# One gated attention and feed-forward block on one core: each engine's instructions kept in the written order, every step in a slot of its own

## The chip, the cores and the metric

The kernel runs on one core of one Trainium2 chip. The metric is the device time of one execution in microseconds, the median of several runs. The engines are named as in the profile: PE (TensorE; PEld its weight loads), DVE (VectorE), ACT (ScalarE), POOL (GpSimd) and SP, whose queue issues most DMAs. POOL issues the indirect DMAs. A line such as L619 is a line of the kernel before.

## The reference, cut to what matters

There are 8 batches of 256 rows, 512 channels, 16 heads of 32; the feed-forward is 1408 wide.

```
x = x + tanh(g_xattn) * xattn(layernorm(x), ctx, mask)
x = x + tanh(g_ffn)   * ffn(layernorm(x))

xattn: q = w8a8_linear(xn, wq, bq)             # rows and weights rounded to int8 with a scale a row
       k = ctx @ wk.T + bk ; v = ctx @ wv.T + bv                            # fp32
       a = softmax(q k.T / sqrt(32) + mask)    # 256 x 256 for each of 16 heads
       return w8a8_linear(a v, wo, bo)
ffn:   xr = x / scale; xr = xr[:, up_reorder_index]       # rows put on an fp8 grid
       g = qlinear(xr, w_gate) ; u = qlinear(xr, w_up)    # columns in down_reorder_index order
       t = silu(g) * u                                    # put on the fp8 grid again, a scale a row
       return qlinear(t[:, down_reorder_index], w_down)
```

The maximum over a row of t (1408 numbers) must be known before that row's grid can be made, and all of attention's output row before it can be rounded to int8.

## The kernel before, in words

Rows are tiled by 128, so a batch has two row tiles. The program is written in a tile framework: its scheduler orders the instructions of each engine when the program is built, from priorities and a timing model of its own, and each engine then works through its queue in that fixed order. The one order that is written by hand is that of the score products and of the head products (`in_turn`).

The outer loop runs over 8 batches of 8 pairs of heads, plus 8 further turns. A turn issues `scores`, `transposed` and `products` of three successive pairs, and then a list of helper steps that `spread` hands out over the turns of a batch: the next batch's norm, keys, values and queries, the last batch's output projection and second norm, a third of the weight pieces in each of batches 0 to 2, and feed-forward steps from batch 3 on.

```
for lag in range(3):
    if 0 <= g - lag < B * NP:
        parts[(g - lag) // NP][lag]((g - lag) % NP)
for f in slots[i]:
    f()
```

The steps and lines that are spoken of below:

| step | lines and tiles |
|---|---|
| softmax of one head | L578 PE scores s (4 banks, one buffer, for 4 heads); L593 DVE sn = -(s + mask) with its row minimum nm; L603 ACT exponential pr with its row sum |
| turning the probabilities | L619 PE transposes t of fp32; L628 DVE (even heads) and L626 ACT (odd heads) copy to pT |
| products with the values | L637 PE poT, four heads in one bank; L651 ACT copy oT; L654 PE transposes po; L658, L660 DVE normalise into o |
| keys, values | L463 PE ct, L466 ACT cT; L473 PE pk, L480 ACT kT; L489 PE pv, L496 DVE v |
| queries | L514 ACT, L522 DVE round; L524 PE qt, L529 copy; L535 PE pq, L542 DVE qT, L545 POOL adds the bias |
| output projection | L299, L300 DVE round o; L687 PE ot, L692 copy; L698 PE py, L706 DVE y; L709, L710 POOL add to x; L711 SP stores x1 |
| second norm | L724 to L729 DVE; L158, L160 ACT and L162, L163 DVE put rows on the fp8 grid; L306 PE transposes tb_x, L309 copy; SP stores scr_x |
| feed-forward, a unit of 352 columns | L752 POOL gathers xg; L775 PE gate and up; L786 DVE scales both; L795 ACT tanh; L796, L797, L798 POOL make tt |
| feed-forward, the end of a row tile | L180 DVE row maximum mxt; L158 to L163 the grid qt; L306 PE tb_t, L309 copy qtT; L828 PE yp; L834 DVE yo; L835 POOL adds x1; SP stores out |
| weight pieces | L395 POOL gathers rows, L401 POOL masks them, then maximum, grid, L306 transposes; the weights go to HBM (scr_gate, scr_up, scr_d) and come back in the wanted order by indirect DMA |

All PE results other than the scores share one ring of four PSUM banks (`bank`, tag m). A row tile of feed-forward has one buffer for tt, qt and qtT each. Copies written `nc.any` may be placed on ACT or DVE by the scheduler. x has four buffers, pr five, pT six, the bf16 rows q8 two, the fp32 rows r_v four.

Of the kernel before, what the change touches and what calls it, by code (L numbers as in the profile page):

```python
# [40 lines left out]
P = 128  # L41
# [8 lines left out]

@with_exitstack
def tile_flamingo_block(
# [22 lines left out]
    nc = tc.nc  # L75
    B, S, C = x.shape
    L = cond.shape[1]
    I = w_gate.shape[0]
    H = 16
# [42 lines left out]
    zeros = ctile([P, IC], "zeros")  # L122
    nc.vector.memset(zeros, 0.0)
    ones = ctile([P, 1], "ones")
    nc.vector.memset(ones, 1.0)
# [25 lines left out]
    held_d = [dram.tile([I, 1], F32, tag=f"held{k}", name=f"held{k}") for k in range(IC)]  # L151
# [3 lines left out]
    def fp8_grid(rp, src, rs, dst, n, name):  # L155

        v = rp.tile([P, n], F32, tag="r_v", bufs=4, name=f"v_{name}")
        nc.scalar.activation(v, src, AF.Identity, scale=rs)  # L158
        a = rp.tile([P, n], FP8, tag="r_a", name=f"a_{name}")
        nc.scalar.activation(a, v, AF.Abs, scale=0.5, saturate=False)  # L160
        q = rp.tile([P, n], FP8, tag="r_q", name=f"q_{name}")
        nc.vector.tensor_scalar(q, v, F8_MAX, -F8_MAX, ALU.min, ALU.max, saturate=False)  # L162
        nc.vector.scalar_tensor_tensor(dst, a, F8_MAX / 2, q, ALU.max, ALU.mult)  # L163

    def scale_of(pool, mx, s, name):

        nc.vector.tensor_scalar(s, mx, R448, None, ALU.mult)  # L167
        rs = pool.tile([P, s.shape[-1]], F32, tag="rs", name=f"rs_{name}")
        nc.vector.reciprocal(rs, s)  # L169
        return rs  # L170

    def int8_scale(pool, mx, s, name):

        nc.vector.tensor_scalar(s, mx, R127, Q_EPS, ALU.mult, ALU.max)
        rs = pool.tile([P, s.shape[-1]], F32, tag="rs8", name=f"rs8_{name}")
        nc.vector.reciprocal(rs, s)
        return rs

    def absmax(dst, src):
        nc.vector.tensor_reduce(dst, src, AX.X, ALU.max, apply_absolute_value=True)  # L180

    with ExitStack() as actx:
# [15 lines left out]

        xt = {}
        norm1, norm2 = {}, {}  # L200

        def load_x(b):
            xt[b] = ld.tile([P, TPB, C], F32, tag="x", name=f"x_{b}", bufs=4)
            nc.sync.dma_start(xt[b], x[b].rearrange("(t p) c -> p t c", p=P))

        def row_tile(b, name, n=1):
            return sm.tile([P, n * TPB], F32, tag=name, name=f"{name}_{b}", bufs=3)

        def norm_stats(b):
            mv = sm.tile([P, TPB, 2], F32, tag="mv1", name=f"mv1_{b}", bufs=3)  # L210
            for nt in range(TPB):
                st = sm.tile([P, 6], F32, tag="st", name=f"st1_{b}_{nt}")
                nc.vector.bn_stats(st, xt[b][:, nt, :])
                nc.vector.bn_aggr(mv[:, nt, :], st)
            norm1[b] = mv

        def norm_roots(b1, b2):

            r = row_tile(b1, "rstd", 2)
            todo = []  # L220
            if b1 < B:
                todo.append((r[:, :TPB], norm1[b1][:, :, 1]))
            if b2 >= 0:
                todo.append((r[:, TPB:], norm2[b2][:, :TPB]))
            for to, var in todo:
                nc.vector.tensor_scalar(to, var, LN_EPS, None, ALU.add)
            ra = r[:, : TPB if b2 < 0 else None] if b1 < B else r[:, TPB:]
            nc.scalar.activation(ra, ra, AF.Sqrt)
            nc.vector.reciprocal(ra, ra)
            if b2 >= 0:  # L230


                s_x = row_tile(b2, "s_x", 2)
                nc.vector.scalar_tensor_tensor(
                    s_x[:, :TPB], norm2[b2][:, TPB:], UNIT, r[:, TPB:], ALU.mult, ALU.mult
                )
                nc.vector.tensor_scalar(s_x[:, TPB:], s_x[:, :TPB], 0.5, None, ALU.mult)
                norm2[b2] = s_x
            if b1 < B:
                nmean = row_tile(b1, "nmean")  # L240
                nc.vector.tensor_scalar(nmean, norm1[b1][:, :, 0], -1.0, None, ALU.mult)
                norm1[b1] = r[:, :TPB], nmean, row_tile(b1, "sx")

        def norm_max(b, nt):
            _, nmean, sx = norm1[b]
            xc = rp.tile([P, C], F32, tag="r_v", bufs=4, name=f"xc_{b}_{nt}")
            nc.scalar.activation(xc, xt[b][:, nt, :], AF.Identity, bias=nmean[:, nt : nt + 1])
            absmax(sx[:, nt : nt + 1], xc)

        def norm_scales(b):  # L250
            rstd, nmean, sx = norm1[b]
            qa, qb = row_tile(b, "qa"), row_tile(b, "qb")
            nc.vector.tensor_tensor(sx, sx, rstd, ALU.mult)
            nc.vector.tensor_scalar(sx, sx, R127, Q_EPS, ALU.mult, ALU.max)
            nc.vector.reciprocal(qa, sx)
            nc.vector.tensor_tensor(qa, qa, rstd, ALU.mult)
            nc.vector.tensor_tensor(qb, qa, nmean, ALU.mult)
            norm1[b] = sx, qa, qb

        def norm_steps(b):  # L260

            steps = [partial(norm_stats, b), partial(norm_roots, b, b - 3)]
            steps += [partial(norm_max, b, nt) for nt in range(TPB)]
            return steps + [partial(norm_scales, b)]


        wT8 = {}
        s8 = {}
        for n, w in (("q", wq), ("o", wo)):
            wT8[n] = wp.tile([P, KC, C], BF16, tag=f"w{n}T", name=f"w{n}T")  # L270
            s8[n] = wp.tile([P, KC], F32, tag=f"s_{n}", name=f"s_{n}")
        wTf = {n: wp.tile([P, KC, C], F32, tag=f"w{n}T", name=f"w{n}T") for n in ("k", "v")}

        def load_halves(n, w, tag):

            halves = []
            for i in range(2):
                wr = kv.tile([P, 2, C], F32, tag=tag, name=f"wr_{n}{i}")
                nc.sync.dma_start(
                    wr, w[i * 2 * P : (i + 1) * 2 * P, :].rearrange("(k p) c -> p k c", p=P)  # L280
                )
                halves.append(wr)
            return [halves[k // 2][:, k % 2, :] for k in range(KC)]

        def prep_fp32(n, rows):
            for k in range(KC):
                wr = rows[k]
                pt = bank(f"pt_{n}{k}")
                for cc in range(KC):
                    nc.tensor.transpose(  # L290
                        pt[:, cc * P : (cc + 1) * P], wr[:, cc * P : (cc + 1) * P], ident
                    )
                nc.scalar.copy(
                    wTf[n][:, :, k * P : (k + 1) * P], pt.rearrange("p (c o) -> p c o", o=P)
                )

        def round_int8(src, rs, dst, name):
            w = rp.tile([P, C], F32, tag="r_v", bufs=4, name=f"ri_{name}")
            nc.vector.tensor_scalar(w, src, rs, MAGIC, ALU.mult, ALU.add)  # L299
            nc.vector.tensor_scalar(dst, w, -MAGIC, None, ALU.add)  # L300

        def transpose_bf16(src, dst, n, name):

            pt = bank(f"tb_{name}", BF16)
            for k in range(n):
                nc.tensor.transpose(  # L306
                    pt[:, k * P : (k + 1) * P], src[:, k * P : (k + 1) * P], ident_b
                )
            nc.any.tensor_copy(dst, pt[:, : n * P].rearrange("p (k o) -> p k o", o=P))  # L309

        def load_rows(n, w, tag, bufs):

            tiles = []
            for k in range(KC):
                wr = at.tile([P, C], F32, tag=tag, name=f"wr_{n}{k}", bufs=bufs)
                nc.sync.dma_start(wr, w[k * P : (k + 1) * P, :])
                tiles.append(wr)
            return tiles

        def prep_int8(n, tiles):  # L320
            for k, wr in enumerate(tiles):
                sk = s8[n][:, k : k + 1]
                absmax(sk, wr)
                rs = int8_scale(sm, sk, sk, f"w{n}{k}")
                qw = at.tile([P, C], BF16, tag="q8", name=f"qw_{n}{k}")
                round_int8(wr, rs, qw, f"w{n}{k}")
                transpose_bf16(qw, wT8[n][:, :, k * P : (k + 1) * P], KC, f"w{n}{k}")

        def row_bcast(dst, cols, name):

            n = cols.shape[-1]
            for k0 in range(0, n, 4):
                m = min(4, n - k0)
                pb = bank(f"rb_{name}{k0}")
# [11 lines left out]
        def held_up():  # L346
# [8 lines left out]
            for k in range(KC):  # L355
# [4 lines left out]
                )  # L360
            nc.vector.tensor_scalar(mu_b, pc, 1.0, None, ALU.min)

        marks = []

        def mark_down(k):

# [636 lines left out]
```

## Time and profile before

| what | us |
|---|---|
| median of three runs | 896.36 |
| lowest, highest | 893.34, 897.14 |
| profiled execution, whole | 906.7 |
| its span | 904.9 |
| first exponential, last exponential of attention | 64.1, 762.8 |
| busy PE, DVE, ACT, POOL | 571.7, 579.7, 443.4, 395.1 |
| mean granted clock of PE | 0.791 of full |

A row of a group of instructions gives line, engine, operation, result and operands, count, busy time and the mean duration of one. A row of waits gives who waited for whom, the sum, the number of times and the longest. A row of stretches gives the stretch, its length, then for each engine the busy time and the number of instructions, the granted clock, the DMA share and GB/s. Rows of the timeline give start, duration, engine, line, operation and operands.

### The profile page before, as it was taken

Reading aid. Unit: us, or ns where it says so; the run is one execution under the profiler, and the core shown is the slowest. Engines: PE = TensorE matmul, PEld = TensorE weight load, DVE = VectorE, ACT = ScalarE, POOL = GpSimd, SP = SyncE. Lnnn points to the kernel's source line nnn. Section 1 sums busy time; section 2 is a strip of 40 time slices with the busy share of each in tenths; the row PEclk is TensorE's granted clock in tenths of the full one; section 3 lists DMA queues with packets and bytes.
Section 4 is the critical chain, followed back from the end, with each engine's and each line's share of the span. In section 5 each row is a group of like instructions: output and inputs, shape, how many; then the busy total and the mean of one; then the engine's idle time right before and its main releaser. Section 6 shows DMA issues by size and latency. Waiting matters only on the chain.

```text
span 904.9 us, 11148 instructions
## 1 busy us (share of the span) xinstructions
PE 571.7 (63%) x3571; PEld 364.4 (40%) x3594; DVE 579.7 (64%) x1645; ACT 443.4 (49%) x1066; POOL 395.1 (44%) x396
## 2 busy tenths in 40 slices
PE   2577785668773679476857677586954765652342
PEld 2436464445542446243524354354533433321121
DVE  3558696597887477646766755866774776555332
ACT  1448675368466464445544543574452545224121
POOL 4374524343300655433625272543617246544650
PEclk9777899787876789677968797887968788765775
DMA  8412132123313301110001101010101001110100
GB/s 258 118 49 64 54 123 88 35 90 138 119 65 124 107 1 48 47 44 21 34 33 58 47 13 36 23 37 12 36 20 40 23 25 40 31 46 12 36 12 13
DMA packets 32898, 50.17 MB, mean 55 GB/s; under 512 B 8411, under 2 KB 15963, under 8 KB 32838
## 3 DMA queue, kind: packets, MB, share of 16 engines
q1 hardware_dynamic: 24598, 36.70, 12.0%
q0 software_dynamic: 4656, 12.21, 4.8%
q10 hardware_dynamic: 3584, 0.54, 0.5%
q8 instruction: 28, 0.46, 0.2%
q14 instruction: 32, 0.26, 0.1%
HBM read 34.55 MB, written 14.88 MB: 55 GB/s over the span
## 4 chain that ended last, share of the span: by engine, by line
PE 26%; POOL 21%; DVE 21%; issue 15%; ACT 10%; DMA 4%; ACTq 1%; another core or an unknown queue 1%; POOLq 0%; DVEq 0%
PE yp L828 6%; POOL tt L798 5%; POOL th L796 5%; POOL th L797 5%; PE pk L473 4%; PE pv L489 3%; PE t L619 3%; DVE mxt L180 3%; DMA wr_gate<-in_L_ffn_w_gate_dram,dd_i 2%; ACT pr L603 2%; DVE sn L593 2%; POOL xg L752 2%; PE poT L637 2%; DVE qt L163 1%; ACT v_t L158 1%
## 5 line engine op out<-in xcount | busy, mean ns | idle before, releaser
L603 ACT ACTIVATE pr<-sn,nm 128x256 f32<-128x256 f32 x256 | 127.9, 501 | 59.3 <-DVE nm L593 21.0
L593 DVE CUSTOM_DVE_ANT_0 sn<-s,mk 128x256 f32<-128x256 f32 x256 | 98.2, 417 | 21.1 <-ACT pr L603 11.4
L795 ACT ACTIVATE th<-gate 128x352 f32<-128x352 f32 x64 | 31.8, 497 | 118.8 <-DVE gate L786 87.4
L619 PE MATMUL t<-ident,pr 128*128 128x128 f32 x512 | 85.9, 322 | 5.6 <-DVE qT L542 4.1
L796 POOL TENSOR_SCALAR th<-th 128x352 f32<-128x352 f32 x64 | 71.4, 1116 | 34.9 <-ACT th L795 26.2
L545 POOL TENSOR_SCALAR qT<-qT,bq_c 128x256 f32<-128x256 f32 x32 | 17.1, 533 | 153.8 <-DVE qT L542 101.6
L473 PE MATMUL pk<-cT,wkT 128*128 128x256 f32 x256 | 71.6, 437 | 17.4 <-ACT cT L466 8.1
L835 POOL TENSOR_TENSOR x<-x,yo 128x512 f32<-128x512 f32 x16 | 20.4, 1276 | 141.1 <-DVE yo L834 140.7
L619 PEld LDWEIGHTS t<-ident,pr 128*128 128x128 f32 x512 | 73.8, 171 | 11.9 <-DVE qT L542 4.3
L306 PE MATMUL tb_t<-ident_b,qt 128*128 128x128 bf16 x176 | 25.0, 301 | 83.3 <-DVE qt L163 81.8
L180 DVE TENSOR_REDUCE mxt<-tt 128x1 f32<-128x1408 f32 x16 | 25.9, 1620 | 76.7 <-POOL tt L798 76.7
L775 PEld LDWEIGHTS <-xg 128*128 128x128 bf16 x512 | 53.3, 105 | 43.5 <-issue 9.8
L473 PEld LDWEIGHTS pk<-cT,wkT 128*128 128x128 f32 x256 | 55.6, 225 | 27.2 <-ACT cT L466 8.3
L828 PE MATMUL yp<-wdT,qtT 128*128 128x512 bf16 x163 | 60.7, 537 | 6.3 <-ACT qtT L309 5.2
L489 PE MATMUL pv<-wvT,cT 128*128 128x512 f32 x128 | 64.1, 648 | 0.5 <-DVE gate L786 0.5
L158 ACT ACTIVATE v_t<-tt,rs_t 128x512 f32<-128x512 f32 (+1 forms) x48 | 31.0, 675 | 67.3 <-DVE rs_t L169 44.0
L797 POOL TENSOR_TENSOR th<-th,gate 128x352 f32<-128x352 f32 x64 | 60.3, 942 | 4.8
L798 POOL TENSOR_TENSOR tt<-th,up 128x352 f32<-128x352 f32 x64 | 59.8, 935 | 4.3
L775 PE MATMUL p_gate<-gateT,xg 128*128 128x352 bf16 x256 | 54.6, 337 | 5.1 <-issue 3.6
L775 PE MATMUL p_up<-upT,xg 128*128 128x352 bf16 x256 | 54.4, 337 | 3.5 <-issue 3.5
L578 PE MATMUL s<-kT,qT 32*128 32x256 f32 x512 | 43.3, 459 | 20.7 <-DVE n L167 8.1
L786 DVE SCALAR_TENSOR_TENSOR gate<-p_gate,s_x,sb_gate 128x352 f32<-128x352 f32 x64 | 37.1, 579 | 29.6 <-POOL th L797 15.0
(193 smaller groups left out, 1350.7 us busy)
## 6 DMA issues: line engine op xcount, KB each, us to landing
x<-x SPq DMA_DIRECT2D x32, 256.0 KB
cr<-in_ctx_dram SPq DMA_DIRECT2D x8, 512.0 KB
x<-in_x_dram SPq DMA_DIRECT2D x8, 512.0 KB
out_dram<-x SPq DMA_DIRECT2D x16, 256.0 KB
wd<-in_L_ffn_w_down_dram SPq DMA_DIRECT2D x4, 704.0 KB
mk<-in_mask_BxSxS_ff_dram SPq DMA_DIRECT2D x8, 256.0 KB
scr_x<-x2T SPq DMA_DIRECT2D x8, 256.0 KB
scr_gate<-gateT SPq DMA_DIRECT2D x1, 1408.0 KB
```

The lines of the kernel that those rows point to most:

```text
L180: nc.vector.tensor_reduce(dst, src, AX.X, ALU.max, apply_absolute_value=True)
L473: nc.tensor.matmul(pk[:, :L], wTf["k"][:, cc, oc * P : (oc + 1) * P], cT[:, cc, :], start=(cc == 0), stop=(cc == KC - 1),)
L489: nc.tensor.matmul(pv, cT[:, cc, lt * P : (lt + 1) * P], wTf["v"][:, cc, :], start=(cc == 0), stop=(cc == KC - 1),)
L578: return nc.tensor.matmul(pss[h][:, nt, :], qT[r0 : r0 + D, oc, nt * P : (nt + 1) * P], kT[r0 : r0 + D, oc, :], start=True, stop=True,)
L593: nc.vector.tensor_tensor_reduce(out=sn[:, nt, :], in0=pss[h][:, nt, :], in1=mk[:, nt, :], scale=-1.0, scalar=3.0e38, op0=ALU.add, op1=ALU ...
L603: nc.scalar.activation(pr[:, nt, :], sn[:, nt, :], AF.Exp, bias=nm[:, nt : nt + 1], scale=-1.0, accum_out=sums[:, nt, h : h + 1],)
L619: nc.tensor.transpose(pst[:, lc, nt * P : (nt + 1) * P], pr[:, nt, lc * P : (lc + 1) * P], ident,)
L775: nc.tensor.matmul(ph[n], xg[0][:, k, nt * P : (nt + 1) * P], wT[n][:, k, cols], start=(k == 0), stop=(k == KC - 1),)
L796: nc.gpsimd.tensor_scalar(th, th, 1.0, None, ALU.add)
L797: nc.gpsimd.tensor_tensor(th, th, scaled["gate"], ALU.mult)
L798: nc.gpsimd.tensor_tensor(h["tt"][:, cols], th, scaled["up"], ALU.mult)
L828: nc.tensor.matmul(py, h["qT"][:, k, :], wdT[:, k, :], start=(k == 0), stop=(k == IC - 1))
```

## The change

`InOrder` wraps each engine; once switched on, it marks every instruction to stay in the order in which it is written, on its engine. The prologue, up to the queries of batch 0, is still ordered by the scheduler.

The loop over turns becomes a loop over 83 slots. The first 64 belong to the 64 pairs of heads. `early(g, step)` and `late(g, step)` enter a step in an agenda, in front of the softmax of slot g or at its end. A slot issues in this order: scores (every other slot, for four heads), early steps, the softmax of its pair, head products of the pair three slots back, transposes of the pair one slot back, normalising of the pair four slots back, late steps. Every chain is cut where it changes engine: a grid, for example, becomes `grid_parts` (ACT), `grid_whole` (DVE) and the transposes (PE), in successive halves of slots.

```diff
+class InOrder:
+    def __getattr__(self, name):
+        method = getattr(self.engine, name)
+        def issue(*args, **kwargs):
+            ins = method(*args, **kwargs)
+            return self.tc.keep_in_program_order(ins) if self.on else ins
+        return issue
...
-for g in range(B * NP + NP):
-    b, i = divmod(g, NP)
-    if i == 0:
-        slots = [[] for _ in range(NP)]
...
-            spread(slots, norm_steps(b + 1), 0, 3)
-            spread(slots, kv_steps, 0, 6)
-            spread(slots, q_steps, 3, 7)
...
-            spread(slots, project_out(b - 1, o_last) + quantise_x2(b - 1), 2, NP)
...
-    for lag in range(3):
-        if 0 <= g - lag < B * NP:
-            parts[(g - lag) // NP][lag]((g - lag) % NP)
-    for f in slots[i]:
-        f()
+for e in (pe, dve, act, pool, sp):
+    e.on = True
+for g in range(max(s for s, _ in agenda) + 1):
+    b, i = divmod(g, NP)
+    if b < B and i % PPC == 0:
+        scores(b, i // PPC)
+    for f in agenda.get((g, 0), []):
+        f()
+    if b < B:
+        softmax(b, i)
+    for lag, f in ((3, weighted), (1, transposed), (4, normalised)):
...
+    for f in agenda.get((g, 1), []):
+        f()
```

A feed-forward row tile and the steps after a batch's attention, with the slots that the rest is built on:

```
# feed_forward(b, nt, g)                      # follow(b, g): projection and second norm
if nt == 0: early(g - 1, gather_x, b)         early(g, rounded)
for j in range(4): late(g + j // 2, unit, j)  late(g + 1, turned)
early(g + 2, scales)                          for nt in range(TPB): late(g + 2, product, nt)
late(g + 2, parts, 0); late(g + 2, parts, 1)  early(g + 3, centred, 0); late(g + 3, parts, 0)
early(g + 3, parts, 2)                        early(g + 4, whole, 0); early(g + 4, centred, 1)
early(g + 3, whole, 0); early(g + 3, whole, 1) late(g + 4, back, 0); late(g + 4, parts, 1)
late(g + 3, turned, 0); late(g + 3, whole, 2) early(g + 5, whole, 1); late(g + 5, back, 1)
late(g + 3, load_x1)                          late(g + 5, store)
late(g + 4, turned, 8); late(g + 5, down)
...
for k in range(IC): up_piece(k, k)            # one gate piece and one up piece a slot, slots 0 to 12
for k in range(KC): down_piece(k, IC + 2 + 2 * k)
for k, (b, nt) in enumerate(ahead): feed_forward(b, nt, 25 + 10 * k // 3)   # batches 0 to 5
for nt in range(TPB):
    feed_forward(B - 2, nt, B * NP + 3 + 3 * nt)
    feed_forward(B - 1, nt, B * NP + 10 + 3 * nt)
```

In batch b's eight slots the next batch's work lies thus: the norm in slots 1 and 2, context transposes late in 0 and 1, keys in 1 and 2, values in 3 and 4, rows of queries in 2 and 3, queries in 4 and 5; the last batch's `follow` starts in slot 3.

Further edits:

- The weights wv and wo are prepared in slots 0 to 2 in place of ahead of the first scores; gate and up pieces are made two a slot in place of one after the other, and their marks (an indirect DMA a piece) with them.
- Copies of turned rows that were `nc.any` are ACT's; of each pair of weight pieces, up's is DVE's. The two normalising products of a group of heads are one instruction.
- Weight loads of w_down are issued by POOL in place of SP. The marks and their zero tables are bf16, and their rows are loaded in slot 10.
- Buffers: x 3, pr 4, pT 5, q8 5, the fp32 rows 4 for ACT's and 2 for DVE's, sn 4 of half the size. The ring of four PSUM banks, the score banks and the single tt, qt and qtT stay.

## The prediction

> **What bounds the kernel now.** I read the page's head first: which engines are busy, the granted clock, the chain that ended last.
>
> ```profile
> span 904.9 us, 11148 instructions
> PE 571.7 (63%) x3571; PEld 364.4 (40%) x3594; DVE 579.7 (64%) x1645; ACT 443.4 (49%) x1066; POOL 395.1 (44%) x396
> PEclk9777899787876789677968797887968788765775
> PE 26%; POOL 21%; DVE 21%; issue 15%; ACT 10%; DMA 4%; ACTq 1%; another core or an unknown queue 1%; POOLq 0%; DVEq 0%
> ```
>
> No engine is above 64%, and the chain passes from engine to engine with none over 26%: the kernel is bound by hand-offs in fixed queues, not by an engine. Second, the span cut at the first exponential (64 us), at batches and at the last one (763 us):
>
> ```profile
> core 0: us, PE busy (x) PEld busy (x) DVE busy (x) ACT busy (x) POOL busy (x), PEclk, DMA share, GB/s
> 64.00:124.00 60.00, 44.44 (x318) 32.08 (x320) 45.98 (x145) 44.12 (x117) 29.56 (x28) 0.86 0.20 61
> 385.00:488.00 103.00, 70.75 (x449) 44.14 (x454) 63.98 (x179) 51.40 (x126) 41.83 (x42) 0.80 0.12 39
> 591.00:675.00 84.00, 61.77 (x407) 40.17 (x403) 57.96 (x172) 46.21 (x118) 37.16 (x38) 0.85 0.07 23
> 763.00:882.00 119.00, 52.94 (x283) 27.32 (x285) 58.35 (x120) 33.38 (x57) 66.27 (x65) 0.69 0.09 29
> ```
>
> A batch (eight pairs of heads) takes 60 us while it carries little else and 84 to 103 us beside feed-forward, though DVE, the fullest, is busy 58 to 64 us of that. Third, the waits, who waited for whom:
>
> ```profile
> PE tb_t L306 <- DVE qt L163: 81.8, 20, 15.1
> DVE mxt L180 <- POOL tt L798: 76.7, 16, 8.6
> DVE yo L834 <- PE yp L828: 50.0, 15, 5.3
> PE tb_x L306 <- DVE q L163: 49.9, 11, 9.9
> PE po L654 <- ACT oT L651: 29.3, 28, 6.1
> PE tb_d L306 <- DVE q_d L163: 20.8, 8, 8.8
> ```
>
> Each is an instruction standing in its queue right behind what makes its operand on another engine: a transpose behind its quantisation, the row maximum behind POOL's last product. Everything queued behind it waits too. Fourth, the timeline, for the pitch of instructions that follow each other (start to start), which is what they occupy:
>
> ```profile
> 61.97 0.42 DVE L593 CUSTOM_DVE_ANT_0 sn<-s,mk 128x256 f32<-128x256 f32 x1
> 62.31 0.42 DVE L593 CUSTOM_DVE_ANT_0 sn<-s,mk 128x256 f32<-128x256 f32 x1
> 873.01 1.09 POOL L796 TENSOR_SCALAR th<-th 128x352 f32<-128x352 f32 x1
> 876.09 1.09 POOL L796 TENSOR_SCALAR th<-th 128x352 f32<-128x352 f32 x1
> ```
>
> sn lasts 417 ns but comes every 345; a unit of feed-forward costs POOL 3.07 us.
>
> **What the Trainium skill says.** (1) "TensorE: Matmul & The Clock Gate", Part 1: TensorE runs at half clock unless recent windows of about 3.4 us were busy. The trace agrees: pitch of the transposes of L619 is 213 ns in half-clock stretches, 109 in full ones; mean granted clock 0.79. (2) Same page, "Architectural detail: the array is 16× 32×32": ScalarE and VectorE are strict first-in-first-out, TensorE pulls only weight loads ahead. The mxt row agrees: 76.7 us with DVE standing. (3) "Perfetto Trace Analysis", "Optimizing Scalar/DVE Operations": an instruction's profiled duration overlaps its successor; 417 against 345 agrees. I count with pitches.
>
> **The change, part by part.** *Work.* It hardly changes. DVE loses the bf16 copies the scheduler gave it (qtT 3.2, x2T 2.5, upT 1.7 of which it keeps half the pieces, qoT 2.8 us) and saves about 2 us by one normalising product in place of two; ACT gains about 10. Counting the written order of the new program with pitches of before (PE at full clock: L619 109 ns, key and value products 216 and 429 per record, gate and up 149, down 216; DVE sn 345, pT 602, gate and up 500, mxt 1540 to 1560, grid 335+602; ACT exponential 400+93) gives for the 64 slots of a pair: PE 358 us (421 at clock 0.85), DVE 449, ACT 363, POOL 318. Table loads (1.28 us each, about 20 before) stay: still one square root per batch.
>
> *Order.* The written order is kept from the first slot on; before it the scheduler still places. A slot has a front (scores, early steps, softmax, lagged transposes and head products) and a back (late steps). The front is DVE's: 320 us of it against PE 112, ACT 186. The back is PE's: 246 at full clock against DVE 129, ACT 177; POOL has 261 there. Worked for slot 26 (batch 3): front DVE = norm_end 1.9 + 4 sn 1.4 + pT 0.6 + normalising 0.45 = 4.4, PE = 8 score records, 8+2 transposes = 1.9; back PE = 2 key products 3.4 + 2 units 2.4 = 5.8, DVE = 4 scalings 2.0, ACT 3.0, POOL 6.0. The fullest engine needs 7.7, both parts one after the other 10.1.
>
> Why they hardly overlap: DVE and ACT empty PE's four ring banks in order, so PE does its front and about one late product, then stands until pT and the copies of that slot are made; DVE reaches its late steps when PE has just begun. So I sum over 64 slots front maximum plus back maximum: 605 us at full clock, 642 at 0.85, 661 at 0.79. I take 0.85 (the windows at 591 and 64 us, where PE was about as full). From it: PE's head start, about 1 us a slot (two transposed heads and one product), -64. Hand-offs inside a slot not hidden, 0.5 us (some four at 0.1 to 0.2 as the short gaps of PE before L828 and L775 show), +32. The row maximum of a tile stands early in the slot after its last two units: POOL ends 7.4 us after the first of these scalings starts (0.5 + 0.5 + 2 x 3.07 + hand-offs), DVE is through after 2.4 and has about 1.8 us of other early steps: 3 us wait less PE's slack, 12 tiles x 2.5 = +30 (56 in this stage before). Square root slots: two table loads in front of the exponentials, 8 x 2.6, half hidden, +10. Sum **650 us**, 10.2 a slot; before 763 - 64 = 699.
>
> *Start.* Scores come right after the queries; before, DVE's qT waited for the transposes of wv (3.0 + 1.7 us) and sn stood behind a weight piece and the next norm until 61.97 though scores ran at 54.85. First exponential about 53 us in place of 64; the moved wv and wo work is in the slots' sums.
>
> *End.* Before, 763.3 to 904.9 = 142 us. After: lags and gather until tile (6,0)'s first unit 14 (4 from the last exponential, 10 through follow's store, gather, landing); its POOL units 12.3; maximum, grids, and the next tile's first unit, because tt has one buffer and PE's transposes stand before the units, 8; (6,1) 12.3; gather of batch 7, 4.2 issue and landing, first unit, 12; (7,0) with one residual addition and half-clock PE 15.6; 8.5; (7,1) 12.3; from its last tt to the end 22.7 as before (882.2 to 904.9). Sum **118**.
>
> *At nothing.* Marks and zero tables in bf16; w_down's loads on POOL's queue (four, in slots where POOL has 1 to 5 us of work); the 11 single-row loads of the marks on SP at slot 10 (before, 16 us of issues from 41 to 57): behind them SP has a load of ctx used four slots later, the two weight stores and x1 stores; if the rows land late, held_down at slot 12 holds PE's queue once, up to 5 us (in the range). SP's other loads and stores stand one to four slots ahead of their users. Smaller rings (x 3, pr 4, pT 5): what frees each stands a slot earlier. POOL's three-operation gathers are 3 us in slots whose POOL sum is 5.6 of about 9; if that cover goes, DVE's mx_gate waits, up to 3 us in 11 slots. Bounds for the hand-offs, which the trace of before does not show in this order: 0 to 1.5 us a slot (0 to 96); for the head start 0 to 2.
>
> Total 53 + 650 + 118 = 821 against its own 904.9 (906.7 with what lies around the span). The median of the runs shown is 896.36, 8.5 under the span, so 821 - 8.5 = **813**.
>
> **Rivals.** (a) *Slots run at their fullest engine.* If four banks and a slot's slack suffice, the sum is of slot maxima: 528 at 0.85, +40 for maxima and table loads = 568; 53 + 568 + 112 - 8.5 = 725. For: slack of a slot between most steps. Against: one ring of four banks for every product. (b) *Slower: the clock.* Every slot has a front in which PE has 1.7 us of work and stands for 2 to 3. If this keeps the clock low, the backs double: two-part sums 755 at 0.6, 838 at 0.5. It decides in the attention slots: break-even is 904.9 - 53 - 118 = 734, that is 726 before corrections, at a mean granted clock of about 0.65. At 0.6: 763, in all 925. For: 0.69 in the tail, where PE is 44% busy. Against: PE would then be over 80% busy and earn full clock back; 0.80 to 0.86 in the batches. (c) *Waits only change place.* Maxima still stand behind POOL and yo behind yp; with 0.9 us of hand-offs (+58), no head start and the +30 the slots take 642 + 58 + 30 = 730: 893. For: those two rows were 127 us before. Against: the four transpose rows are separated by at least half a slot now.
>
> **How the numbers follow.** Forecast 0.66, (a) 0.14, (b) 0.12, (c) 0.08, split evenly between slower by more and the rest. About 0.5%, 4.5 us, is what a measurement of this kernel can tell from no change (three runs lie within 3.8 us). Forecast and (a) are faster: 0.80; within 0.5% 0.04; slower 0.16. The range takes (a)'s upper half to just above no change: 740 to 905; without (b) and (c) the forecast's own is 760 to 870.
>
> **What would show it.** Right: first exponential near 53 us, batches of 75 to 90 us each, the transpose rows of the waits (tb_t, tb_x, tb_d) down to a few us, DVE near 65 to 70% of the stage, PE standing in fronts with pT or a copy as releaser, mxt <- tt still 30 to 50 us. Wrong: clock under 0.7 between 53 and 700 us (b); batches under 72 us (a); mxt or yo waits over 100 us (c).

## The result and the profile after

The changed kernel takes 934.79 us, median, against 896.75 for the kernel before on the same chip: a ratio of 1.042 (95% interval 1.037 to 1.047). It is **slower by 4%**, where 813 was predicted. The profiled execution took 933.0 us, 931.2 of them its span. In the profile of a kernel with `InOrder` nearly every instruction bears the line of the wrapper (L61, or L62 where an experiment added a line), so it is read by tiles.

The head of the page, the same rows as before:

```profile
span 931.2 us, 11038 instructions
PE 583.0 (63%) x3570; PEld 366.7 (39%) x3591; DVE 605.6 (65%) x1590; ACT 463.2 (50%) x1092; POOL 402.7 (43%) x400
PEclk9978877887878598778987699888878777677775
DVE 34%; PE 25%; POOL 15%; ACT 11%; issue 9%; DMA 3%; another core or an unknown queue 1%; POOLq 0%; DVEq 0%; ACTq 0%; SPq 0%
```

The mean clock (0.798; 0.791 before) is what it was, and the engines' busy times are up by 2 to 5%. Of the chain, DVE's share has grown most, from 21 to 34%. The stretches, with the columns as before, are batches 0, 4 and 6 and the end:

```profile
38.30:135.20 96.90, 63.12 (x374) 41.29 (x373) 73.20 (x200) 54.74 (x130) 54.90 (x49) 0.82 0.21 63
411.50:517.10 105.60, 67.98 (x436) 41.87 (x439) 66.74 (x179) 49.72 (x124) 47.40 (x47) 0.86 0.10 33
610.30:712.10 101.80, 70.34 (x437) 44.34 (x439) 66.49 (x179) 51.21 (x126) 40.45 (x42) 0.82 0.07 24
797.70:905.00 107.30, 56.82 (x277) 29.48 (x282) 58.57 (x120) 43.40 (x76) 63.94 (x62) 0.73 0.11 35
```

By its first and last exponential the execution splits into 39 us of start (64 before), 760 of slots (699) and 132 of end (142). Start and end gained 35 us, the slots lost 61. The loss lies in batches 0 to 2, which carry the weight pieces: 97, 93 and 92 us, counted from first sn to first sn, against 61, 73 and 80; the other five, up to the last sn, together take 5 us more than before. (By sn the slots lost 72 us; before, the last exponential came 13 us after the last sn, now 1.) Part of it is moved work, since weights that were prepared ahead of the first scores are now made in the slots. The two rows are batches 0 to 2, before and after:

```profile
62.00:276.20 214.20, 155.03 (x1028) 106.71 (x1029) 168.54 (x510) 139.35 (x353) 77.59 (x73) 0.83 0.27 86
```

```profile
38.30:319.40 281.10, 181.72 (x1123) 120.79 (x1124) 199.06 (x552) 159.18 (x386) 107.13 (x102) 0.79 0.25 82
```

DVE is busy there for 31 us more, and for 14 less ahead of them. But even from the beginning of the execution to the end of batch 2 it is 319 us, where it was 276, and in no batch of the changed kernel was an engine busy for more than 76% of the time. So the answer is in the waits:

```profile
ACT pr L61 <- DVE nm L61: 249.9, 51, 12.9
...
DVE mxt L61 <- POOL tt L61: 56.7, 14, 6.3
PE tb_t L61 <- DVE qt L61: 52.0, 15, 14.6
...
DVE gate L61 <- PE p_gate L61: 43.2, 27, 5.0
DVE yo L61 <- PE yp L61: 41.7, 11, 7.0
PE tb_up L61 <- DVE pT L61: 34.2, 9, 5.6
...
PE tb_x L61 <- DVE q L61: 9.6, 10, 2.9
```

The rows that the change was cut for did go: tb_x 49.9 to 9.6, and of tb_t's 52.0 only 7.5 are in the slots. New ones stand in their place. PE products of every sort (tb_up is one of a dozen) stand for DVE's **pT**, which must empty a bank of their ring: summed over the slots 163 us of the 253 in which PE waited. DVE, in turn, stands before the instructions that take PE's late products (gate, yo, v; called takers below). Both happen in one slot of the timeline:

```profile
525.51 0.75 DVE L61 SCALAR_TENSOR_TENSOR yo<-yp,sy,sd_b 128x512 f32<-128x512 f32 x1 [5.60 <-PE yp L61]
...
531.78 0.69 DVE L61 COPY pT<-t 128x512 f32<-128x512 f32 x1
...
532.52 3.78 PE L61 MATMUL pk<-cT,wkT 128*128 128x256 f32 x8 [3.30 <-DVE pT L61]
...
538.37 0.58 DVE L61 SCALAR_TENSOR_TENSOR gate<-p_gate,s_x,sb_gate 128x352 f32<-128x352 f32 x1 [4.97 <-PE p_gate L61]
```

From 525.5 to 533 DVE does the norm's statistics, two grids, four sn and pT without a pause, and PE stands for 3.3 us of it; then PE runs its products and DVE stands for 5. The two engines take turns.

### The profile page after: what moved, and what is told of

Same layout as the page of the kernel before. It is cut to its first block, busy times and chain, and to the rows that moved or that the text cites. A ratio compares the mean times of both kernels' runs of the same rounds, so it can differ in the third digit from the quotient of the medians.

```text
span 931.2 us, 11038 instructions
## 1 busy us (share of the span) xinstructions
PE 583.0 (63%) x3570; PEld 366.7 (39%) x3591; DVE 605.6 (65%) x1590; ACT 463.2 (50%) x1092; POOL 402.7 (43%) x400
## 4 chain that ended last, share of the span: by engine, by line
DVE 34%; PE 25%; POOL 15%; ACT 11%; issue 9%; DMA 3%; another core or an unknown queue 1%; POOLq 0%; DVEq 0%; ACTq 0%; SPq 0%
POOL th L61 8%; PE pk L61 6%; DVE sn L61 6%; PE pv L61 5%; POOL tt L61 4%; ACT pr L61 4%; PE yp L61 3%; DVE mxt L61 3%; POOL x L61 2%; PE p_gate L61 2%; DVE pT L61 2%; DVE qt L61 2%; DVE up L61 2%; PE p_up L61 2%; DVE q_up L61 1%
## 5 line engine op out<-in xcount | busy, mean ns | idle before, releaser
L61 ACT ACTIVATE pr<-sn,nm 128x256 f32<-128x256 f32 x256 | 126.9, 497 | 255.1 <-DVE nm L61 249.9
L61 POOL TENSOR_SCALAR th<-th 128x352 f32<-128x352 f32 x64 | 73.4, 1146 | 186.0 <-ACT th L61 142.2
L61 DVE CUSTOM_DVE_ANT_0 sn<-s,mk 128x256 f32<-128x256 f32 x256 | 92.8, 418 | 13.9 <-remote 8.1
L61 PE MATMUL pk<-cT,wkT 128*128 128x256 f32 x256 | 77.4, 464 | 30.4 <-DVE pT L61 14.8
L61 PEld LDWEIGHTS <-xg 128*128 128x128 bf16 x512 | 58.0, 115 | 58.8 <-issue 17.3
L61 PE MATMUL t<-ident,pr 128*128 128x128 f32 x512 | 78.7, 302 | 3.5 <-ACT x2T L61 1.4
L61 PEld LDWEIGHTS pk<-cT,wkT 128*128 128x128 f32 x256 | 58.3, 236 | 44.5 <-DVE pT L61 16.8
L61 PEld LDWEIGHTS t<-ident,pr 128*128 128x128 f32 x512 | 62.2, 154 | 32.3 <-issue 12.2
L61 PE MATMUL p_gate<-gateT,xg 128*128 128x352 bf16 x256 | 63.2, 378 | 16.3 <-DVE pT L61 13.1
L61 DVE SCALAR_TENSOR_TENSOR gate<-p_gate,s_x,sb_gate 128x352 f32<-128x352 f32 x64 | 37.3, 582 | 49.4 <-PE p_gate L61 43.2
L61 PE MATMUL pv<-wvT,cT 128*128 128x512 f32 x128 | 68.0, 680 | 1.2 <-ACT qtT L61 0.4
L61 POOL TENSOR_SCALAR qT<-qT,bq_c 128x256 f32<-128x256 f32 x32 | 15.8, 499 | 117.7 <-DVE qT L61 117.3
L61 POOL TENSOR_TENSOR th<-th,gate 128x352 f32<-128x352 f32 x64 | 61.3, 958 | 5.3
L61 PE MATMUL tb_t<-ident_b,qt 128*128 128x128 bf16 x176 | 21.5, 266 | 66.1 <-DVE qt L61 52.0
L61 DVE TENSOR_REDUCE mxt<-tt 128x1 f32<-128x1408 f32 x16 | 25.9, 1619 | 56.7 <-POOL tt L61 56.7
L61 POOL TENSOR_TENSOR tt<-th,up 128x352 f32<-128x352 f32 x64 | 60.5, 945 | 5.0
L61 PE MATMUL yp<-wdT,qtT 128*128 128x512 bf16 x162 | 51.3, 462 | 17.3 <-DVE pT L61 7.9
L61 ACT ACTIVATE th<-gate 128x352 f32<-128x352 f32 x64 | 31.7, 496 | 59.0 <-DVE gate L61 51.0
L61 PE MATMUL poT<-pT,v 128*32 128x256 f32 x512 | 45.9, 449 | 23.7 <-DVE nm L61 13.5
L61 PE MATMUL p_up<-upT,xg 128*128 128x352 bf16 x256 | 59.9, 366 | 0.9 <-DVE gate L61 0.9
L61 POOL TENSOR_TENSOR x<-x,yo 128x512 f32<-128x512 f32 x16 | 21.0, 1311 | 82.1 <-DVE yo L61 67.2
L61 PE MATMUL s<-kT,qT 32*128 32x256 f32 x512 | 41.8, 445 | 19.1 <-DVE nm L61 19.1
```

The source lines that it names most:

```text
L61: ins = method(*args, **kwargs)
```

## The experiments

Ratios are to the kernel before, timed on the same chip; the changed kernel's is 1.042. Where an expectation speaks of theory A, that is: pT stands too late in DVE's queue. In this section the slots' length is from the first sn to the last: 759 us in the changed kernel, 688 before.

**Lagged steps first.**

```diff
 scores(b, i // PPC)
+for lag, f in ((3, weighted), (1, transposed), (4, normalised)): ...
 for f in agenda.get((g, 0), []): f()
 softmax(b, i)
-for lag, f in ((3, weighted), (1, transposed), (4, normalised)): ...
```

> In a slot the lagged steps (head products of the pair three back, transposes of the pair one back, normalising) are issued right behind the scores, ahead of the early steps and the softmax, so DVE's pT copy stands in front of the early steps and the four sn and not behind them. Theory A (the slots are long because pT waits behind DVE's early steps and sn and holds PE's bank, after which DVE stands behind PE's late products): PE's waits on pT fall from about 160 us to under 60, the 64 slots get shorter by 40 to 90 us, in all 850 to 900. Theory B (the slots are long for the row maxima and scales, mxt 57 us, and other hand-offs between late steps and the next early ones): 925 to 940, only the names of the waits change. Theory C (the edits of buffers and copies, not the order, made it slower): also 925 to 940.

Measured: 883.6 us, ratio 0.995 (0.992 to 0.997); slots 713. That is the gain of theory A, though the run with pT freed, below, takes its reason away. DVE now waits 96.5 us for the transposes themselves (pT for t), but its wait before gate fell from 43 to 18.5 us and before yo from 42 to 13: PE makes its late products while DVE does early steps and sn.

**No written order at all** (`e.on = False`).

> The same program with the marking never switched on: the framework's scheduler orders every engine. Theory C (edits other than the order cost the time): 925 to 945 as with the order. Theory A and B (the written order costs it): 870 to 905, no slower than the kernel before, since the scheduler moves pT and the scales to where they are ready.

Measured: 797.3 us, ratio 0.900 (0.897 to 0.904); slots 630, mean clock of the whole execution 0.85. Lower than either range. The edits are not what costs: the same program in the scheduler's order is 10% faster than the kernel before. The written order alone turns that into a loss of 4%.

**Two more banks.** Scores are made for a slot's two heads in two banks, and the ring gets the two that come free.

```diff
-ps_m = ...tile_pool(name="ps_m", bufs=4, space=PSUM)
+ps_m = ...tile_pool(name="ps_m", bufs=6, space=PSUM)
-heads = range(oc * HPC, (oc + 1) * HPC); four = ps_s.tile([P, HPC, TPB, L], ...)   # every second slot
+heads = (2 * i, 2 * i + 1);              two = ps_s.tile([P, 2, TPB, L], ...)       # every slot
```

> Order as in the changed kernel, but the scores are made for the two heads of a slot, in two banks in place of four, and the ring of PE's other results has six banks in place of four. Theory A: PE may run two more products ahead while pT waits, its waits on pT fall to about half, 870 to 905. Theory B: 925 to 940. A loss against B of up to 10 us can come from scores of two heads that share less of the array than four.

> The control of the run with six banks: scores for the two heads of a slot in two banks, everything in the written order, but the ring of PE's other results keeps its four banks (two banks lie idle). If the depth of the ring made that run fast, 915 to 945, like the changed kernel. If it was the earlier or shorter score products, 835 to 870.

Measured with six banks: 837.0 us, 0.945 (0.940 to 0.949); with the same scores and four banks: 931.5 us, 1.043 (1.036 to 1.051), no different from the changed kernel. The control met its first range, and the run with six banks fell below its own. So the depth of the ring is worth 10 hundredths of the time before, in an unchanged written order. The slots of the two as one stretch each, six banks first, then four:

```profile
35.00:703.40 668.40, 513.74 (x3169) 331.30 (x3185) 513.98 (x1409) 395.32 (x986) 317.43 (x313) 0.84 0.18 57
```

```profile
35.90:795.10 759.20, 536.84 (x3174) 342.93 (x3174) 523.52 (x1409) 400.19 (x986) 320.14 (x313) 0.82 0.15 50
```

The same work in 668 us and in 759: with six banks PE waits 151 us in the slots (216 in the control, 253 in the changed kernel) and DVE 135 (216 in both). Both engines' waits shrink together. That fits two engines that wait for each other; by itself it doesn't prove it, since any shorter stretch with the same work has less waiting.

**The order of DVE freed, or kept alone.**

```diff
-for e in (pe, dve, act, pool, sp):
+for e in (pe, act, pool, sp):     # free_dve
+for e in (dve,):                  # dve_only
     e.on = True
```

> Order kept on PE, ACT, POOL and SP, while DVE's instructions are placed by the scheduler. Theory A: most of the loss is in DVE's written order, 870 to 905. Theory B or the other engines' order: 920 to 945.

> The written order is kept on DVE alone, the other engines are the scheduler's. If DVE's written order is what costs, 900 to 935, near the changed kernel. If the loss needs the written order on both sides (PE's products in a fixed order too), 820 to 870.

Measured: 801.1 us, 0.904 (0.900 to 0.907), with DVE free, below either range and hardly more than with all engines free (0.900). With DVE alone in order 889.0 us, 0.993 (0.990 to 0.995), between the two ranges. DVE's queue is what must not be in this order; but if the others may move around it, 5 of the 14 hundredths between 1.042 and 0.904 go as well. So it lies in the pairing of DVE's order with that of the others. Which of PE, ACT and POOL it is paired with was not tried one by one.

**Which instructions of DVE.** Here each instruction of an engine is pinned behind the last pinned one, and single kinds are left out of the chain. All other instructions, and all other engines, keep their written order; the traces of these runs show PE, ACT and POOL in the changed kernel's sequence.

```diff
-return self.tc.keep_in_program_order(ins) if self.on else ins
+if self.on and not self.free: ...  # pinned behind self.last
...
-dve.tensor_copy(pT, pst)                       # f1
+dve.freed(dve.tensor_copy)(pT, pst)
-dve.tensor_tensor_reduce(out=sn, ...)          # f2, f23
+dve.freed(dve.tensor_tensor_reduce)(out=sn, ...)
-dve.scalar_tensor_tensor(scaled[n], ph[n], ...)  # f3, f23; likewise v, qT, y, yo
+dve.freed(dve.scalar_tensor_tensor)(scaled[n], ph[n], ...)
```

> Every instruction keeps the written order of the changed kernel, except DVE's pT copies (one a slot), which the scheduler may place; they move forward by some 10 to 20 places in about a third of the slots, and no other engine's order changes. If pT behind early steps and sn is the main loss (theory A in its narrow form), 860 to 890. If what matters is that sn stands behind other DVE work, so that ACT, the transposes and all of the next slot start late (theory A2), 905 to 925. If it is DVE's late steps that stand before PE's products are made (theory A3), 910 to 930.

Measured: 933.3 us, 1.043 (1.039 to 1.046), outside every range named. The edit did move pT (36 of the 64 stand earlier in DVE's sequence, by up to 16 places), and it gained **nothing**. This run pins instructions in another way than the changed kernel does and takes the same time, so the way of pinning is not what costs. The waits of this run:

```profile
ACT pr L62 <- DVE nm L62: 251.1, 51, 13.3
...
DVE gate L62 <- PE p_gate L62: 45.8, 29, 5.3
...
PE ct L62 <- DVE pT L62: 17.8, 4, 6.3
```

In the slots PE's waits for pT fell from 163 us to 62, and all its waits together stayed at 253: ACT's copy oT came in as releaser (5 to 39), and DVE's v, st and grids. The rows for pr and gate stand where they stood. The narrow theory A is wrong. pT was only the name on the wait. A likely reason: of the three banks that PE's front holds, ACT frees two (oT and the odd head's pT), and those copies stand behind four exponentials, which stand behind four sn. This is read from the written order and fits the releasers; it was not tried by itself.

> As the changed kernel, except that DVE's sn may be placed by the scheduler: most sn of four heads then stand together, right after their scores, ahead of the early steps of their slots and of late steps of the slot before. Theory A2: 820 to 870. Narrow A (pT): 900 to 930, since pT keeps its place behind the early steps, though the sn of the same slot are no longer in front of it. A3: 910 to 930.

> As the changed kernel, except that the DVE instructions that take PE's late products (gate and up scalings, v, qT, y, yo) may be placed by the scheduler; most move back by a few places, some behind the next slot's first steps. A3: 860 to 890. Narrow A and A2: 915 to 935.

> As the changed kernel in the order of PE, ACT, POOL, SP and of all of DVE but two kinds: sn, and the instructions that take PE's late products (gate and up scalings, v, qT, y, yo), which the scheduler may place. If these two kinds are what DVE's written order costs, 800 to 815, as with all of DVE free (801). If other steps (norms, grids, maxima, pT) matter too, 830 to 865. If both act on one coupling so that freeing one is enough, 865 to 880.

Measured: sn free 871.2 us, 0.973 (0.970 to 0.976), slots 701. Takers free 880.9 us, 0.983 (0.979 to 0.987), slots 714. Both free 815.2 us, 0.920 (0.914 to 0.925), slots 651. The first is a little above its range for A2, the second inside that for A3, the third at the upper edge of its first. In the trace 161 of the 256 sn stand earlier and none later; more than half of the takers stand later, most by one or two places. These are two losses of about equal size, 7 and 6 hundredths of the time before, and they nearly add (12). Together they make up most of the 14 that DVE's order costs; the remaining 2 belong to other steps, lie in batches 0 to 2 (242 us there, 225 with all of DVE free) and were not split further. With sn free, ACT's wait for nm halves, from 250 to 128 us. The gains do not lie where the changed kernel fell behind: of the 58 us that sn brings, 48 are in batches 3 to 7, and of the takers' 46 us 27.

**sn moved by hand.** In every second slot the softmax of both pairs comes right behind the scores.

```diff
+if b < B and i % PPC == 0:
+    softmax(b, i)
+    softmax(b, i + 1)
 for f in agenda.get((g, 0), []): f()
-if b < B:
-    softmax(b, i)
```

> Everything in a written order, but another one: in every second slot the softmax of both pairs (eight sn, eight exponentials) is issued right behind the scores, ahead of the early steps; the other slots have none. If it is the place of sn that matters and not that the order is fixed, 850 to 885, like the run in which only sn was free. If a written order as such costs, since no place suits every slot, 905 to 935. A loss of its own is possible: the eight exponentials need pr buffers that the transposes of the slot give back.

Measured: 882.8 us, 0.989 (0.981 to 0.997). This is inside the first range: a written order is not slow as such, for this one, as fixed as the other, is 5% faster. Its gain, too, is all in batches 3 to 7; batches 0 to 2 take 283 us as against 281.

**Combinations.**

> Written order on all engines, with the lagged steps ahead of the early steps and a ring of six banks. If both act on one coupling, 815 to 840, little better than six banks alone (837); if they add, 785 to 805.

Measured: 897.0 us, 1.005 (1.003 to 1.008): neither range. It is worse than six banks alone by 6%, and worse than the lagged steps first with four. Two rows say where it went:

```profile
DVE pT L61 <- PE t L61: 125.4, 56, 6.0
PE s L61 <- DVE nm L61: 83.9, 24, 8.8
```

With the lagged steps first, DVE's first work in a slot needs PE's transposes, which stand in PE's queue behind all late products of the slot before. More banks let PE's products run ahead, but DVE waits for their end all the same (96.5 us with four banks). The second row (33.2 us in the run with the lagged steps first and scores for four heads) is the price of the two banks: scores now have room for one slot's heads only, and the next ones wait until the softmax has read them. A run with four banks and scores for two heads in this order was not made, so the two are not separated.

> Both at once: scores for two heads, ring of six banks, and the order of every engine left to the scheduler. If written order and a shallow ring are two sides of one coupling (PE and DVE take turns), freeing both brings little over freeing the order alone, 780 to 800. If they are separate losses, their gains add: 700 to 740.

> The same two kinds free, scores for two heads, ring of six banks. If nothing else in the written order costs, 780 to 800, like six banks with the whole order free (786). If the written order of PE and ACT still costs, 805 to 837.

Measured: order free and six banks 786.5 us, 0.881 (0.874 to 0.887); only sn and takers free and six banks 785.7 us, 0.888 (0.882 to 0.894), each in its first range. These two are the fastest kernels here, 11 to 12% under the one before. Six banks are worth 10 hundredths in the written order, 3 once sn and takers may move, 2 when all may: the ring's depth and the place of DVE's steps are mostly two cures for one ailment.

> The kernel before, with scores for two heads and a ring of six banks, its order the scheduler's as before. If the ring's depth matters because the written order makes PE and DVE take turns, it brings little here, 870 to 895. If four banks hold up any order alike, 790 to 830, the same 10 per cent as in the written order.

Measured: 888.8 us, 1.0025 (0.999 to 1.006), in the first range. But this run does not isolate the ring. The scheduler made a new order for it, and the two banks were taken from the scores. PE's waits for those, in the kernel before and in this run:

```profile
PE s L578 <- DVE nm L593: 8.0, 6, 3.3
```

```profile
PE s L576 <- DVE nm L591: 74.3, 18, 10.6
```

In the slots PE's waits in all fell from 214 us to 181, while the dearer scores (see the last section) raised its busy time from 472 to 502. What six banks would bring here without that price was not tried: no control with four banks was run.

## Why the prediction was wrong, point by point

**The bound now** was read rightly for the slots beside feed-forward: hand-offs in fixed queues. It holds for the changed kernel too. Two readings under it were not right. PE, not DVE, is the fullest engine in the rows at 385 and 591 us (70.75 and 61.77 us busy). And batch 0, the one of 60 us, does not carry little: batches 0 to 2 make the weight pieces, and DVE was busy for 77, 74 and 84% of them. There was least to gain there, and there the change put more work.

**Start.** Said: first exponential at 53 us; measured: 39. The step was right, its size too small by 14 us: the first scores ran at 37.0 us in place of 54.9, 18 us earlier, where 4.7 had been counted. **End.** Said 118, measured 132. The first maximum of tile (6,0) started 35 us after the last exponential, not 26, and that of (6,1) 62, not 47; from there on the steps ran as counted. The two errors cancel by luck.

**The slots** hold the whole error: 760 us in place of 650. That a slot has two parts, with PE standing in the first and DVE in the second, came as predicted. Against the working, term by term:

- *Two-part sum* (front maximum plus back maximum), taken at clock 0.85: 642. In the slots it was 0.81, which by the same sums (661 at 0.79) gives about 655: +13.
- *Row maxima* +30: measured 36 (mxt in the slots): +6. *Table loads* +10: 16 loads in the slots where there were 14 before; left as it was.
- **"PE's head start, about 1 us a slot, −64" and "Hand-offs inside a slot not hidden, 0.5 us, +32" are the failed steps.** What remains is 760 − 655 − 36 − 10 = 59 us, 0.9 a slot with no head start at all, where −32 was counted: +91.

13 + 6 + 91 is the 110, by construction: the 59 is what is left over and not a measurement of hand-offs. (Worked by its own rule, slot 26 is 10.4 and not 10.1, since POOL's 6.0 is the fullest of the back; this is small.) Part of the 59 may be DVE's own: it was busy 524 us in the slots, where pitches had counted 449, and 480 with its order free; sn lasts 417 ns but comes every 345 in a row, so an instruction that stands alone counts with its whole duration. The runs don't separate the two. The head start was real for PE: in the slot shown it did the transposes and one key product ahead of pT. But it was counted as time off the slot, and an engine's lead shortens the slot only if the one that it feeds is not tied back to it. DVE's takers stood right behind pT, so DVE reached them when PE had only just begun the rest, and its next sn stood behind the takers. The two runs with takers or sn free show what these two ties cost: 46 and 58 us of slots; the run with six banks shows that a real lead of PE was to be had and was worth 91. (That this equals the +91 above is chance.)

The Trainium skill fits this. Its page "Perfetto Trace Analysis", "Optimization Strategy", says that one gap that repeats over a stretch can mean too little PSUM for the next tile; here it did, 0.945 against 1.043 with four banks. The same page, "Matmul Optimizations", asks that all eight PSUM banks be used; the kernel before used all eight, and another split of them left its time as it was (1.0025). Strict queues on DVE, quoted in the prediction, were taken into account for what stood behind mxt, and not for what stood behind the takers.

**The next wait.** The prediction said that PE would stand with pT or a copy as releaser. That was right as an observation (163 us) and wrong as a cause (the run with pT freed).

**Edits at nothing** (marks, loads, buffers): no run isolates them, but with the same edits and the scheduler's order the kernel takes 0.900, so they are not the loss. Why they gain 10% there was not tried; by the traces 58 us of it are in the slots, and the rest at both ends.

**Rivals.** (a), slots at their fullest engine, is out for this order; with six banks, sn and takers free, the slots take 618 us, still over its 568. (Its sum takes 112 us for the end where the forecast takes 118, and gives no reason.) (b), the clock, is out: 0.81 in the slots. (c), waits only change place, came nearest: no head start, and 0.9 us of hand-offs. That 0.9 is left over here too is partly luck, since the 59 us may hold time of DVE's own, and its reason was not what happened: the rows of maxima and yo fell from 127 us to 98. It was priced at clock 0.85 and without the 10 us for table loads, and so at 893 and not 903, and it was held unlikely because the rows tb_t and tb_x would go. They went; what came was not in those rows. Its test, mxt or yo over 100 us, did not fire (56.7 and 41.7), since it looked for the old waits.

**Signs named.** Came: tb_x, tb_d (no wait for its grid is left) and, in the slots, tb_t down, mxt at 36 us in the slots, DVE at 69% of the slots (524 of 759), pT as releaser. Did not: the first exponential near 53 us (39), which was even earlier, and batches of 75 to 90 us (86 to 106). All signs named for "right" but these two also hold in a kernel that is slower; of the two, only the batch length pointed to a slower one.

## What to carry to other kernels

When two engines stand for each other within one period, sum up each one's waits before and after a repair: if the named wait goes and the sum stays (163 to 62 us, and 253 both times), the name was not the cause. In a written order, count an engine's lead as a gain only after asking where the instruction that takes its product stands, and what stands behind that one; take it as late as the buffers allow, and put what feeds other engines (here sn) ahead of everything that waits. Buffers between two engines are worth what the order makes of them: two banks took 10 hundredths off here, 3 in a better order, none in the kernel before, where PE waited for the scores' banks from which they were taken.

## What was not expected of the hardware

Scores for two heads at a time cost PE twice the time of four. The 512 products, four heads together in the changed kernel, then two:

```profile
L61 PE MATMUL s<-kT,qT 32*128 32x256 f32 x512 | 41.8, 445 | 19.1 <-DVE nm L61 19.1
```

```profile
L61 PE MATMUL s<-kT,qT 32*128 32x256 f32 x512 | 85.5, 458 | 37.3 <-DVE nm L61 37.3
```

Each lasts the same (445 and 458 ns), but four rather than two share the array, as the Trainium skill's page "TensorEngine Tiling (Array Packing)", "Theoretical Speedup", allows for 32 rows: up to four times. Here four at a time took half of what two at a time took. PE's busy time rose by 36 us and the kernel's time did not move (1.043 against 1.042). In the slots PE's waits fell by as much, from 253 us to 216: it had that much room.
